# Order of the first strip's projections in a fused window-attention and depthwise-convolution kernel

## The chip, the cores and the metric

The kernel runs on one core of a Trainium2 chip. The metric is device time in microseconds (us): the median of a few executions of the same program. Engines are named TensorE (PE in the profile, its weight loads PEld), VectorE (DVE), ScalarE (ACT), GpSimd (POOL) and SyncE (SP), which here only issues transfers.

## The reference

The input x has 16 images of 56 x 56 tokens with 384 channels, in float32. Two layers follow each other, each with a residual.

```python
# layer 0: shifted-window attention on a group norm of x (32 groups)
qkv = roll(gn(x)) @ w_qkv.T                    # 12 heads of 32 channels, windows of 7 x 7 tokens
score = q @ k.T / sqrt(32) + rel_pos + masks
out = softmax(score) @ v
x = x + roll_back(out @ w_out.T + b_out)
# layer 1: depthwise 3 x 3 convolution with binarised weights on a group norm
x = x + depthwise(gn(x), sign(clip(w)))
```

The mean and variance of a group run over the whole image, so the attention of an image starts only when all of it has been read.

## The kernel before, in words

**Tiling.** An image is cut into 8 strips of 7 rows (`NS`); a strip `s` holds 8 windows, or 392 tokens (`ST`), and the whole run has 128 strips. A strip is worked on in two units of four windows each (`UPS`, `UW`); `u` counts units over the run. Channels lie on partitions in three blocks of 128 (`NC`), so the projections of a strip are six blocks of queries and keys and three of values, each block three products of 128 x 128 by 128 x 392 that add up in one bank of PSUM. Of each such float32 product the profile shows two records.

**Functions of one strip.**
- `normalize(s)` (ScalarE, L463) writes the normalised strip into `xn`, of which there is one buffer. It has to wait until the projections of the strip before have read it.
- `query_key(s, m)` (TensorE, L474) makes one block of queries or keys in a bank `pq`; ScalarE copies it to `qk` (L481).
- `value(s, m)` (TensorE, L487) makes a block of values in a bank `pv`; ScalarE copies it to `vt` (L494).
- `turn(s, m)` (VectorE, L498) transposes that block in squares of 32 x 32 from `vt` to `vq`.
- `by_key(s, part)` (SP, L510) carries `vq` to the tile `v`, in which keys lie on partitions. It issues eight transfers for each of its two parts, sixteen for a strip; each reads what all three turns of the strip wrote.

**Functions of one unit.**
- `scores(u)` (TensorE, L529) writes queries times keys into the score banks, of which there is one set.
- `softmax(u)` (VectorE, L546) adds the bias to them and writes `e`; the bias tile was made before, by `add_bias` (VectorE, L230), out of `rel` and `mask`, which POOL loads (L210, L213, L218).
- `exponential(u)` (ScalarE, L564) takes the exponential of `e`.
- `add_up(u)` (TensorE, L599) sums it over the keys, `invert(u)` (ScalarE and VectorE, L637 to L640) makes the reciprocal.
- `attend(u)` (TensorE, L619) multiplies `e` with `v` into two banks `po`, 96 small products; ScalarE copies them (L629) and `divide(u)` (VectorE, L647) scales them.
- `project(s, m)` (TensorE, L658, every second unit) makes the output projection, to which VectorE adds x (L666).

**What sets the order.** The whole program is under `tc.manual_schedule()`: each engine does its instructions in the order in which the Python code emits them, and waits at each one for the data and buffers it needs. `all_units` is the written-out order. It first emits the first strip by hand, and then runs a loop over units. In the loop `heavy(u)` gives six slots of projection work for the next strip: values and their turns in the first unit of a strip, with `by_key` near its end, and the rest of queries and keys in the second. The scores and the softmax of the next unit are emitted between the slots, and the unit's own sums and `attend` after slot 0:

```python
for m in range(NC):
    if half == 0 and more:
        todo[m].append((value, (s + 1, m)))
        todo[m + 1].append((turn, (s + 1, m)))
        todo[NC + m].append((query_key, (s + 1, m)))
```

Light work (the convolution of the image before, loads of the next image) is put into the slots by due times that `plan` hands out with `at(when, f, ...)`. `fetch_halves` (POOL, L421) loads strips of the next image into `xl`, and `turn_halves` (VectorE, L438) takes them up; the first 24 of these loads are issued in unit 0. In the queues of POOL and SP they and `by_key` stand where the code emits them, too.

Ahead of `all_units` the program reads the first image, loads weights and bias, gathers the statistics (through DRAM, SP L287 and L289) and normalises strip 0. `all_units` stands twice in the program; the second call, with `fast` false, lies under a condition on the numbers' range.

Of the kernel before, what the change touches and what calls it, by code (L numbers as in the profile page):

```python
# [34 lines left out]
def kernel(  # L35
# [17 lines left out]
    NC = C // P  # L53
# [39 lines left out]
    def bank(name):  # L93
        return ps.tile([P, 512], F32, tag="mm", name=name)
# [365 lines left out]
    def normalize(s):  # L460
        coef = coefs[0, s // NS]
        for c in range(NC):
            nc.scalar.activation(  # L463
                xn[:, c, :, :T],
                xs[s][:, c, :].rearrange("p (w t) -> p w t", t=T),
                AF.Identity,
                bias=coef[:, c, 1:2],
                scale=coef[:, c, 0:1],
            )

    def query_key(s, m):
        pq = bank(f"pq_{s}_{m}")
        for c in range(NC):
            nc.tensor.matmul(  # L474
                pq[:, :ST].rearrange("p (w t) -> p w t", t=T),
                wq_t[:, c, m * P : (m + 1) * P],
                xn[:, c, :, :T],
                start=(c == 0),
                stop=(c == NC - 1),
            )  # L480
        nc.scalar.copy(qk[:, m, :ST], pq[:, :ST])  # L481

    def value(s, m):

        pv = bank(f"pv_{s}_{m}")
        for c in range(NC):
            nc.tensor.matmul(  # L487
                pv[:, :ST].rearrange("p (w t) -> p w t", t=T),
                wq_t[:, c, 2 * C + m * P : 2 * C + (m + 1) * P],
                xn[:, c, :, :T],  # L490
                start=(c == 0),
                stop=(c == NC - 1),
            )
        nc.scalar.copy(vt[:, m, :, :T], pv[:, :ST].rearrange("p (w t) -> p w t", t=T))  # L494

    def turn(s, m):

        nc.vector.transpose(  # L498
            vq[:, :, :, m].rearrange("p h n d -> p n h d"),
            vt[:, m].rearrange("p (n w) (j b) -> p n (w j) b", w=2, b=D),  # L500
        )

    def by_key(s, part):

        if part == 0:
            vs[s] = vpool.tile([P, NW // 2, C], F32, tag="v", name=f"v_{s}")
        v = vs[s]
        for half in range(2 * part, 2 * part + 2):
            for i in range(HPC):
                nc.sync.dma_start(  # L510
                    v[half * D : (half + 1) * D].rearrange("k n (m c) -> k (n m) c", m=NC)[:, :, i * D : (i + 1) * D],
                    vq[i * D : (i + 1) * D, half].rearrange("k n m d -> k (n m) d"),
                )

    def scores(u, fast):


        s, n = divmod(u, UPS)
        pp = score_banks
        rows = T if fast else HT  # L520
        for j in range(NC):
            for r in range(2):
                for k in range(2 * HPC):
                    i, w = k % HPC, (k + k // HPC) % 2
                    part = slice(i * D, (i + 1) * D)
                    q0 = (n * UW + 2 * r + w) * T
                    row, col = (w, r) if fast else (r, w)
                    k0 = (2 * j + col) * T
                    nc.tensor.matmul(  # L529
                        pp[row * HT : row * HT + rows, i, k0 : k0 + T],  # L530
                        qk[part, NC * fast + j, q0 : q0 + rows],
                        qk[part, NC * (not fast) + j, q0 : q0 + T],
                        start=True,
                        stop=True,
                    )
        raw[u] = pp

    def softmax(u, fast):

        s = u // UPS  # L540
        pp = raw[u]
        e = es.rearrange("k (i j) w q -> k i (j w) q", i=HPC)[:, :, :, :T]
        if fast:
            flat = es.rearrange("k h w q -> k (h w q)")[:, : NH * 2 * T]
            e = flat.rearrange("k (i n q) -> k i n q", i=HPC, q=T)
        nc.vector.scalar_tensor_tensor(  # L546
            e,
            pp[:, :, : NC * 2 * T].rearrange("q i (n k) -> q i n k", k=T),
            QSCALE,
            bias[:, int(s % NS == NS - 1)].rearrange("q (i j) w k -> q i (j w) k", i=HPC),  # L550
            ALU.mult,
            ALU.add,
        )
        if fast:
            return
        e = es.rearrange("q h w k -> q (h w) k")[:, :, :T]
        top = small.tile([P, 2 * NH], F32, tag="top", name=f"top_{u}")
        nc.vector.tensor_reduce(top, e, AX.X, ALU.max)
        nc.vector.tensor_tensor(e, e, top.unsqueeze(2).to_broadcast([P, 2 * NH, T]), ALU.subtract)

    def exponential(u, fast):
        if fast:
            flat = es.rearrange("k h w q -> k (h w q)")[:, : NH * 2 * T]
            nc.scalar.activation(flat, flat, AF.Exp, accum_out=reach[:, 0, u : u + 1])  # L564
            return
        e = es.rearrange("q h w k -> q (h w) k")[:, :, :T]
        nc.scalar.activation(e, e, AF.Exp)
        total = small.tile([P, 2 * NH], F32, tag="total", name=f"total_{u}")
        nc.vector.tensor_reduce(total, e, AX.X, ALU.add)
        inv = small.tile([P, 2 * NH], F32, tag="inv", name=f"inv_{u}")  # L570
        nc.vector.reciprocal(inv, total)
        nc.vector.tensor_tensor(e, e, inv.unsqueeze(2).to_broadcast([P, 2 * NH, T]), ALU.mult)
# [366 lines left out]
    def heavy(u):  # L939

        s, half = divmod(u, UPS)
        todo = [[] for _ in range(2 * NC)]
        more = s + 1 < B * NS
# [5 lines that stand above are left out]
            if half and more:  # L949
                todo[m].append((query_key, (s + 1, NC + m)))  # L950
            if half:
                todo[NC + m].append((project, (s, m)))
        if more and not half:
            for part in range(2):
                todo[NC + 2 * part].append((by_key, (s + 1, part)))
        if half and s + 2 < B * NS:
            todo[NC + 1].append((normalize, (s + 2,)))
        return todo
# [5 lines left out]
    def plan(last_queue):  # L964
        for b in range(1, B):
            plan_load(b)
            plan_conv(b - 1, NU * b, 2.6 if b < B - 1 else 1.95, 3, 0.4, nc.gpsimd)
        at(B * NU - 6, fetch_late)
        for t in range(9):
            at(B * NU - 5 + 0.3 * t, diagonal, t)  # L970
        plan_last(B - 1, B * NU)

    def all_units(fast):
        for m in range(2 * NC):
            query_key(0, m)
        scores(0, fast)
        softmax(0, fast)
        for m in range(NC):
            value(0, m)
        normalize(1)  # L980
        exponential(0, fast)
        for m in range(NC):
            turn(0, m)
        for part in range(2):
            by_key(0, part)
        plan(nc.sync)
        for u in range(B * NU):
            todo = heavy(u)
            light = [(w, f, a) for w, f, a in sorted(side.pop(u, []), key=lambda i: i[0])]
            more = u + 1 < B * NU  # L990

            then = NC if u % UPS else NC - 1
            for i in range(len(todo)):
                run(todo[i])
                if i == 0:
                    if fast:
                        add_up(u)
                    else:
                        for j in range(NC):
                            transpose(u, j)  # L1000
                    if fast:
                        invert(u)
                    attend(u, fast)
                    if fast:
                        divide(u)
                if i == then and more:
                    scores(u + 1, fast)
                    softmax(u + 1, fast)
                if i == then + 1 and more:
                    exponential(u + 1, fast)  # L1010
                while light and light[0][0] - u <= (i + 1) / len(todo):
                    _, g, a = light.pop(0)
                    g(*a)
            for _, g, a in light:
                g(*a)
        for _, g, a in sorted((i for u in side for i in side[u]), key=lambda i: i[0]):
            g(*a)
        side.clear()
# [110 lines left out]
```

## Time and profile before

| what | value |
| --- | --- |
| time, median of 3 runs | 4079.17 us (4078.88 to 4080.06) |
| the profiled execution's own time | 4081.16 us |
| span of its trace | 4079.4 us |
| instructions | 144987 |
| TensorE busy | 3981.1 us |
| VectorE busy | 3495.8 us |
| ScalarE busy | 2231.7 us |
| GpSimd busy | 1870.2 us |
| mean granted TensorE clock | 0.991 |
| moved by DMA | 438.93 MB, 108 GB/s on average |

The span starts with the first recorded instruction of the program and ends with the last; the profiled execution's own time holds what lies around it as well. Times in the timeline and in the chain of waits count from the start of the span. A line of the timeline gives start, duration, engine, line, operation, the tiles it writes and reads, the number of records that are merged into it, and, in brackets, the idle time of the engine ahead of it with what ended it. In a table of slices each engine's busy time stands with its number of instructions, and after the five engines come the granted TensorE clock (1.00 is full speed), the mean busy share of the 16 DMA engines, and GB/s. The name of a releaser is inferred from semaphores, and can be that of another transfer which used the same semaphore.

### The profile page before, as it was taken

To read this page: it belongs to the slowest core of one execution; us is meant where nothing else is said; L and a number is where in the kernel's file an instruction comes from. 1 tells how busy PE (TensorE), PEld (TensorE's weight loads), DVE (VectorE), ACT (ScalarE), POOL (GpSimd) and SP (SyncE) were. 2 spreads that over 40 slices of the span, in tenths; PEclk is the share of its full clock that TensorE was granted. 3 is DMA by queue.
4 is the path that set the end of the run, shared out by engine and by line. 5 is a ranking of instruction groups with operands and counts; after the bars stand their busy time and mean duration, and the time that the engine had idled before them with its cause. 6 is when DMAs were issued, how large, how long until landed. Compare 5 with 4: busy or idle time off the path is not lost.

```text
span 4079.4 us, 144987 instructions
## 1 busy us (share of the span) xinstructions
PE 3981.1 (98%) x63161; PEld 2447.1 (60%) x63161; DVE 3495.8 (86%) x3712; ACT 2231.7 (55%) x4654; POOL 1870.2 (46%) x3165
## 2 busy tenths in 40 slices
PE   5999999999999999999999999999999999999997
PEld 3666666656656666566666666666566566666656
DVE  4555989889898998989889898998989889898897
ACT  2555646555565655656555565655656556565552
POOL 5444535545453554545445452554545455452100
PEclk8999999999999999999999999999999999999998
DMA  4434556655665665556665665655556565664544
GB/s 95 78 62 90 112 102 127 107 109 107 114 114 111 117 111 108 111 99 128 108 116 104 113 117 105 117 117 101 115 101 123 105 124 104 108 123 79 108 102 110
DMA packets 1523990, 438.93 MB, mean 108 GB/s; under 512 B 1458970, under 2 KB 1473979, under 8 KB 1523346
## 3 DMA queue, kind: packets, MB, share of 16 engines
q1 hardware_dynamic: 1432680, 267.66, 38.9%
q0 software_dynamic: 87648, 159.12, 16.4%
q8 instruction: 500, 8.19, 0.9%
q10 hardware_dynamic: 3018, 2.78, 0.3%
q14 instruction: 144, 1.18, 0.1%
HBM read 169.63 MB, written 158.46 MB: 80 GB/s over the span
## 4 chain that ended last, share of the span: by engine, by line
PE 46%; issue 16%; POOL 12%; DVE 12%; DMA 7%; SPq 4%; ACT 2%; DVEq 0%; ACTq 0%; POOLq 0%
PE pq L474 19%; PE pv L487 10%; PE py L658 8%; POOL xl L421 8%; DVE o L786 5%; PE score_banks L529 3%; PE po L619 3%; SPq L510 3%; DMA xl<-in_x_dram 2%; PE score_banks L599 2%; DMA mvd<-mv 2%; DVE e L546 1%; POOL dev L270 1%; DMA gt<-mvd 1%; DVE xt L438 1%
## 5 line engine op out<-in xcount | busy, mean ns | idle before, releaser
L474 PE MATMUL pq<-xn,wq_t 128*128 128x392 f32 x4608 | 1586.7, 497 | 0.1
L421 POOL DMA_DIRECT2D xl<-in_x_dram x1980 | 1329.3, 722 | 153.8 <-DVE xt L438 94.2
L786 DVE SCALAR_TENSOR_TENSOR o<-hp,dw_t,o 128x1568 f32<-128x1568 f32 x752 | 1378.4, 1833 | 5.7 <-DVE o L786 0.5
L474 PEld LDWEIGHTS pq<-xn,wq_t 128*128 128x128 f32 x4608 | 846.1, 188 | 596.1 <-issue 1.4
L487 PE MATMUL pv<-xn,wq_t 128*128 128x392 f32 x2304 | 815.9, 497 | 9.8 <-DVE y L666 8.6
L658 PE MATMUL py<-ot,wo_t 128*128 128x392 f32 x2304 | 818.2, 500 | 4.8 <-DVE ot L647 3.8
L481 ACT COPY qk<-pq 128x392 f32<-128x392 f32 x768 | 368.4, 482 | 609.6 <-PE pq L474 609.3
L678 POOL COPY y<-y 128x63 f32<-128x63 f32 x128 | 59.4, 464 | 1280.5 <-DVE y L666 1280.5
L487 PEld LDWEIGHTS pv<-xn,wq_t 128*128 128x128 f32 x2304 | 424.2, 189 | 309.9 <-DVE y L666 10.4
L658 PEld LDWEIGHTS py<-ot,wo_t 128*128 128x128 f32 x2304 | 425.8, 190 | 306.5 <-DVE ot L647 20.1
L564 ACT ACTIVATE e<-e 128x1176 f32<-128x1176 f32 x256 | 303.3, 1185 | 462.5 <-DVE e L546 461.4
L639 DVE SCALAR_TENSOR_TENSOR ln<-score_banks,inv 128x588 f32<-128x588 f32 x256 | 195.9, 765 | 349.2 <-ACT inv L638 349.2
L494 ACT COPY vt<-pv 128x392 f32<-128x392 f32 x384 | 188.8, 492 | 393.0 <-PE pv L487 392.1
L619 PEld LDWEIGHTS po<-e,v 49*32 49x32 f32 x24576 | 352.2, 105 | 60.4 <-issue 14.3
L619 PE MATMUL po<-e,v 49*32 49x49 f32 x24576 | 347.1, 212 | 13.4 <-DMA v<-vq 11.9
L546 DVE SCALAR_TENSOR_TENSOR e<-score_banks,bias 128x1176 f32<-128x1176 f32 x256 | 347.2, 1356 | 10.7 <-PE score_banks L529 10.7
L529 PEld LDWEIGHTS score_banks<-qk 32*49 32x49 f32 x24576 | 265.7, 118 | 145.4 <-issue 108.9
L450 ACT COPY x<-xt 128x196 f32<-128x196 f32 x720 | 225.5, 368 | 176.0 <-DVE xt L438 175.6
L529 PE MATMUL score_banks<-qk 32*49 32x49 f32 x24576 | 298.2, 218 | 2.6 <-DVE ln L639 2.2
L498 DVE STREAM_TRANSPOSE vq<-vt 128x512 f32<-128x512 f32 x384 | 265.6, 693 | 9.9 <-ACT vt L494 6.4
L463 ACT ACTIVATE xn<-x,coef 128x392 f32<-128x392 f32 x384 | 247.1, 711 | 13.3 <-DMA coef<-cod 13.3
L666 DVE TENSOR_TENSOR y<-py,x 128x392 f32<-128x392 f32 x384 | 213.3, 555 | 43.1 <-PE py L658 39.2
(174 smaller groups left out, 3279.3 us busy)
## 6 DMA issues: line engine op xcount, KB each, us to landing
v<-vq SPq DMA_DIRECT2D x2048, 48.0 KB
xb<-mid SPq DMA_DIRECT2D x90, 855.5 KB
out_dram<-o SPq DMA_DIRECT2D x736, 98.0 KB
mid<-y POOLq DMA_DIRECT2D x112, 619.5 KB
xl<-in_x_dram POOLq DMA_DIRECT2D x1260, 52.5 KB
mid<-y POOLq DMA_DIRECT2D x15, 354.0 KB
xl<-in_x_dram POOLq DMA_DIRECT2D x180, 28.0 KB
mid<-y POOLq DMA_DIRECT2D x15, 265.5 KB
```

Of the source, the lines that this page charges most:

```text
L421: nc.gpsimd.dma_start(xz[i * D + lo : i * D + hi, c, k : k + n, :], flat[token : token + n * (hi - lo)].rearrange("(k t) c -> t k c", k=n) ...
L463: nc.scalar.activation(xn[:, c, :, :T], xs[s][:, c, :].rearrange("p (w t) -> p w t", t=T), AF.Identity, bias=coef[:, c, 1:2], scale=coef[: ...
L474: nc.tensor.matmul(pq[:, :ST].rearrange("p (w t) -> p w t", t=T), wq_t[:, c, m * P : (m + 1) * P], xn[:, c, :, :T], start=(c == 0), stop=( ...
L481: nc.scalar.copy(qk[:, m, :ST], pq[:, :ST])
L487: nc.tensor.matmul(pv[:, :ST].rearrange("p (w t) -> p w t", t=T), wq_t[:, c, 2 * C + m * P : 2 * C + (m + 1) * P], xn[:, c, :, :T], start= ...
L498: nc.vector.transpose(vq[:, :, :, m].rearrange("p h n d -> p n h d"), vt[:, m].rearrange("p (n w) (j b) -> p n (w j) b", w=2, b=D),)
L529: nc.tensor.matmul(pp[row * HT : row * HT + rows, i, k0 : k0 + T], qk[part, NC * fast + j, q0 : q0 + rows], qk[part, NC * (not fast) + j, ...
L546: nc.vector.scalar_tensor_tensor(e, pp[:, :, : NC * 2 * T].rearrange("q i (n k) -> q i n k", k=T), QSCALE, bias[:, int(s % NS == NS - 1)]. ...
L564: nc.scalar.activation(flat, flat, AF.Exp, accum_out=reach[:, 0, u : u + 1])
L619: nc.tensor.matmul(po[w][i * D : (i + 1) * D, (2 * j + r) * T : (2 * j + r + 1) * T], vs[s][keys, n * 2 + r, h * D : (h + 1) * D], by_head ...
L658: nc.tensor.matmul(py[:, :ST], wo_t[:, c, m * P : (m + 1) * P], ots[s][:, c, :], start=(c == 0), stop=(c == NC - 1),)
L786: nc.vector.scalar_tensor_tensor(acc, by_half(hp[:, dy : dy + BR, dx : dx + W]), dw_t[:, c, t : t + 1], acc, ALU.mult, ALU.add)
```

## The change

The blocks with which `all_units` starts, for strip 0, are put in another order. Before, queries and keys came first, then the scores and softmax of unit 0, the values, `normalize(1)`, the exponential of unit 0, the turns, and `by_key`. After, each value block is emitted with its turn behind it, then come both parts of `by_key`, then queries and keys, scores, softmax, `normalize(1)` and the exponential. No call is added or removed, and the loop over units is as it was.

```diff
     def all_units(fast):
+        for m in range(NC):
+            value(0, m)
+            turn(0, m)
+        for part in range(2):
+            by_key(0, part)
         for m in range(2 * NC):
             query_key(0, m)
         scores(0, fast)
         softmax(0, fast)
-        for m in range(NC):
-            value(0, m)
         normalize(1)
         exponential(0, fast)
-        for m in range(NC):
-            turn(0, m)
-        for part in range(2):
-            by_key(0, part)
         plan(nc.sync)
```

## Prediction, made before the result was known

> **What bounds the kernel now.** I read the page first, then the list of TensorE's waits, then the timeline and the chain of waits around the strip that the change touches, then slices of 1 us there.
>
> The page's first part says which engine the whole run hangs on:
>
> ```profile
> PE 3981.1 (98%) x63161; PEld 2447.1 (60%) x63161; DVE 3495.8 (86%) x3712; ACT 2231.7 (55%) x4654; POOL 1870.2 (46%) x3165
> ```
>
> TensorE is idle for only 4079.4 - 3981.1 = 98 us. The waits of TensorE say where some of that lies; the second fence is the same view limited to 300 to 3800 us.
>
> ```profile
> PE po L619 <- DMA v<-vq: 11.9, 15, 5.4
> ...
> PE pv L487 <- ACT xn L463: 1.2, 1, 1.2
> ```
>
> ```profile
> PE pv L487 <- DVE y L666: 8.6, 13, 0.7
> PE po L619 <- DMA v<-vq: 4.0, 11, 0.6
> ```
>
> Of the 11.9 us that `attend` (po, L619) waits for the values' transfers, 4.0 lie in the long middle part; the rest (7.9) is the first unit. In 3500 us of middle TensorE waits under 14 us in all, so whatever TensorE gains at the start it keeps: nothing there has slack that could swallow it. The timeline of the start (start, duration, engine, line):
>
> ```profile
> 60.27 13.78 PE L474 MATMUL pq<-xn,wq_t 128*128 128x392 f32 x36
> ...
> 66.85 5.85 DVE L230 TENSOR_TENSOR bias<-rel,mask 128x147 f32<-128x147 f32 x16 [6.44 <-DMA xl<-in_x_dram]
> ...
> 75.05 6.19 PE L487 MATMUL pv<-xn,wq_t 128*128 128x392 f32 x18
> ...
> 84.81 0.73 PE L599 MATMUL score_banks<-e,ones 49*32 49x294 f32 x16
> ...
> 96.43 6.57 PE L487 MATMUL pv<-xn,wq_t 128*128 128x392 f32 x12
> ...
> 128.94 4.22 PE L487 MATMUL pv<-xn,wq_t 128*128 128x392 f32 x12
> ```
>
> The reader is to see three things. TensorE's sums (L599) are done at 85.54, and the next dense work starts after `attend` at 96.43. The same twelve records of `value` take 6.57 us after that hole and 4.22 us later: the clock had fallen. And VectorE adds the bias until 72.70. The chain of waits names what fills the hole:
>
> ```profile
> 81.81 0.72 DVE vq L498
> 82.55 0.76 SPq L510
> ...
> 93.07 2.11 DMA v<-vq
> 95.22 1.28 PE po L619 x76
> ```
>
> `turn` of the last block ends at 82.53; SP then issues the 16 transfers of `by_key` one by one, the last at 93.07, which lands 2.11 us later: 12.63 us from first issue to last landing. The slices tell the clock (7th number) and the DMA share (8th):
>
> ```profile
> 86.00:87.00 1.00, 0.00 (x0) 0.00 (x0) 0.00 (x0) 0.97 (x2) 0.00 (x0) 1.00 0.63 93
> 88.00:89.00 1.00, 0.00 (x0) 0.00 (x0) 0.79 (x2) 0.00 (x0) 0.00 (x0) 0.50 0.33 49
> ```
>
> **What the Trainium skill says.** "TensorE: Matmul & The Clock Gate", Part 1, has a clock at half after an idle window of about 3.4 us, back after a busy one, with windows that run free of the program. The trace agrees: half clock from about 87.5 to 101.2. It also shows that a window need not be quite idle: TensorE worked some 1.4 us between 84.1 and 87.5. "DMA: Bandwidth & Descriptors", Latency and other measured facts, gives a fixed cost of about 2 us a transfer; here 2.11 us. "Trainium Kernel Development and Optimization", Key Constraints, says that transfers issued from SP and POOL run on the same 16 DMA engines and interleave. That bears on the change, which moves `by_key` under POOL's fetch of x.
>
> **The change, part by part.** It removes and adds no instruction; three blocks of TensorE and what hangs on each change places.
>
> *TensorE's order.* Before: queries and keys 13.78, scores 1.07, values 6.14, ending at 81.24. After: values, queries and keys, scores. The same work at the same clocks must end at about 81.3 again. The first block pays for the cold clock and the arrival of xn: eighteen products took 13.78 where twice the nine of `value` would be 12.38, so 1.40 goes to whoever is first. Values then end at 60.27 + 6.19 + 1.40 = 67.86, queries and keys at 80.24, scores at 81.3. Cost nothing.
>
> *ScalarE's queue.* Three vt copies of 0.49 now stand before the six qk copies, each under products that take about 2 us per block. `normalize(1)` waits for the last reader of xn, now the last key block (80.24) instead of the last value block (81.24), so it comes 1.0 us earlier.
>
> *VectorE's queue.* The vt copies are done at about 68.4, but `turn` stands behind the sixteen additions of the bias in a queue that keeps its order. Those wait until 66.85 for rel and mask (the profile names POOL's later transfer, but L230 reads only these two) and run to 72.70. Three turns of 0.71 with their gaps: 72.70 + 2.2 = 74.9. That is the new start of `by_key`, 82.53 - 74.9 = 7.65 us earlier. Behind the turns on VectorE stands the softmax of unit 0; it is ready only when the scores end (81.3), so the turns cost it nothing while the bias is done by 79.
>
> *SP's queue.* All 16 issues of `by_key` move too. Ahead of them is only the coefficients' load (57.37), and nothing else is on SP until the next strip. Last issue 74.9 + 10.52 = 85.4, last landing 87.55, if the train keeps its pace.
>
> *The collision.* POOL issues 24 fetches of x from 64.94 to 81.67. Before, the train started after them; now 7 of its 12.6 us lie beside them. Alone the fetches hold the DMA engines at 0.39 (65 to 82 us), the train with its tail 0.45 (83 to 95). The sum, 0.84, is under one. A later strip shows both together: from 137 to 149 us, with 12 fetches, share 0.85, SP's 16 issues took 11.33 us where the uncontended ones run from 82.55 to 93.69, 11.14. Lower bound: nothing. Upper bound: SP's train at 1602 to 1617 us, beside stores, took 8 issues in 6.65 and 8 in 6.72 where 5.3 is normal, so +2 us here with slower landings. I take 0.5, since the last 4 us of the train have the DMA engines alone.
>
> *What is late next.* Without the values' wait TensorE would be ready for `attend` when? Softmax at 81.4 to 82.8, exponential at 82.85 (before 83.50), sums 1.31 later at 84.16, done at 84.9. The values land at 87.55 to 88, so they still end the wait; the rest of the hole is about 3 us instead of 10. `attend` ends 1.28 after the last landing: 88.85, before 96.50; gain 7.65, with the collision 7.15.
>
> *The clock.* The hole cost 6.57 - 4.22 = 2.35 us more in slow products. A hole of 3 us with some of `attend`'s products in it fits inside a window or is shared by two. Bounds: nothing saved (0) and all saved (2.35). I take 2.35: in any window at least a third would be busy, and the window before it is full. But the fall at 87.5 after a window about 40% busy shows that this is not certain.
>
> *Sum:* 7.65 - 0.5 + 2.35 = 9.5 us. The profiled execution took 4081.16 (span 4079.4 and 1.8 around it): 4071.7. The median of the timed runs is 2.0 under that, so 4079.17 - 9.5 = **4069.7 us**.
>
> **Rivals.** *A, smaller gain:* the collision costs its 2 us, the clock falls nonetheless, or both: gains of 5.6 to 8, 4071.2 to 4073.5; taken as 4072.5. For it: the share of 0.85, where any further load saturates; the fall after a 40% window. *B, given back:* the wait moves to something that doesn't come earlier with TensorE, as the fetched x for the next batch, which `turn_halves` takes at 116.91. Against it: those fetches are issued by 81.67, 27 us before even the earlier need. Gain 0: 4079.2. *C, slower:* `by_key`'s train and POOL's fetches choke each other, because every issue of SP from the ninth on waits for an older transfer to land. It decides when the train takes over 95.2 - 74.9 = 20.3 us instead of 12.6. At double the pace, 16 x 1.31 + 2.1 = 23.1, it lands at 98.0: +2.8, 4082.0; to lose 0.2% it would have to take 28.5. For it: single issues of 1.4 to 2 us on SP; against it the 11.33 of a train under the same fetches.
>
> **How the numbers follow.** Forecast 0.74, A 0.16, B 0.05, C 0.05. A measurement of this kernel can tell about 0.2%, 8.2 us, from no change: below 4071.0 is faster. The forecast's cases (8.2 to 11) are on that side, and a little of A: 0.75. Most of A, all of B and the nearer part of C are within 0.2%: 0.22. C's tail: 0.03. The low end takes the full gain with no collision, 10.0, and 1.5 for a shift of windows and of the small waits of the middle (0.7 at most each): 4067.7. The high end takes A whole: 4074.0.
>
> **What would show it.** First L510 at about 74.9, last near 85.5, sixteen of them in 11 to 12 us (right); `turn` directly behind the bias at 72.7; softmax of unit 0 at 81.4, as before the sums; TensorE's wait for v near 3 us; `value` after `attend` in 4.2 us, without half clock. It is wrong if v lands after 90, if the clock is half at 89 to 92, if the turns wait for something other than the bias, or if the shift at 130 us isn't found at 3900 us.

## The result and the profile after

The changed kernel takes 4071.55 us (median of 15 runs, 4068.01 to 4074.75), the kernel before 4079.27 in the same measurement: 7.7 us less, ratio 0.998 with a 95% interval of 0.9972 to 0.9988. Two more measurements, each beside runs of the kernel before on the same chip, gave 0.9981 (0.9973 to 0.9989; 8.4 us) and 0.9977 (0.9967 to 0.9986; 9.4 us). The same kernel differs by about 4 us from one chip to another, so medians are compared within one measurement, on one chip. The profiled execution took 4072.83 us, with a span of 4071.0.

The page's first part: TensorE's busy time hardly changed (3981.1 before), the span did.

```profile
PE 3978.3 (98%) x63161; PEld 2445.6 (60%) x63161; DVE 3495.6 (86%) x3712; ACT 2236.0 (55%) x4654; POOL 1876.6 (46%) x3165
```

TensorE's waits over the whole run, and then in 300 to 3800 us:

```profile
PE po L619 <- DMA v<-vq: 7.3, 16, 2.4
```

```profile
PE pv L487 <- DVE y L666: 8.4, 13, 0.9
PE po L619 <- DMA v<-vq: 5.0, 15, 0.9
```

The wait for v was 11.9 us in all; outside the middle it fell from 7.9 to 7.3 - 5.0 = 2.3, and the longest single wait from 5.4 to 2.4. The middle waits nearly as before: all of TensorE's listed waits there add up to 15.4 us, against 13.8. The timeline of the start:

```profile
59.11 7.71 PE L487 MATMUL pv<-xn,wq_t 128*128 128x392 f32 x18
...
65.73 5.86 DVE L230 TENSOR_TENSOR bias<-rel,mask 128x147 f32<-128x147 f32 x16 [6.47 <-DMA mask<-in_wmask_dram]
...
66.66 12.01 PE L474 MATMUL pq<-xn,wq_t 128*128 128x392 f32 x36
...
71.50 1.89 DVE L498 STREAM_TRANSPOSE vq<-vt 128x512 f32<-128x512 f32 x3
...
82.57 0.73 PE L599 MATMUL score_banks<-e,ones 49*32 49x294 f32 x16 [0.46 <-ACT e L564]
...
85.68 2.10 PE L619 MATMUL po<-e,v 49*32 49x49 f32 x94 [2.35 <-DMA v<-vq]
...
87.71 5.09 PE L487 MATMUL pv<-xn,wq_t 128*128 128x392 f32 x12
```

Three turns run in one piece directly behind the bias. The hole between the sums and `attend` is 2.35 us. But `value` behind it still takes 5.09 us, not 4.22: the clock fell again. The chain of waits and the slices (clock in the 7th column of numbers):

```profile
71.59 1.81 DVE vq L498 x3
73.42 0.76 SPq L510
...
82.37 3.18 DMA v<-vq
85.68 2.10 PE po L619 x90
```

```profile
86.00:87.00 1.00, 1.00 (x51) 0.97 (x52) 0.58 (x1) 0.00 (x0) 0.00 (x0) 0.55 0.03 4
88.00:89.00 1.00, 1.00 (x2) 0.55 (x2) 0.45 (x1) 0.52 (x2) 0.00 (x0) 0.50 0.00 0
90.00:91.00 1.00, 1.00 (x5) 0.56 (x4) 0.00 (x0) 0.14 (x1) 0.00 (x0) 1.00 0.00 0
```

Before, the half clock lasted from 87.5 to 101.2; now from about 86.1 to 89.5. In the second and third trace of the changed kernel it lasted from 88.4 to 91.8 and from 87.7 to 91.1.

The first projection starts at a slightly different place in each trace (58 to 61 us), through loads that the change doesn't touch. So the start is compared by counting from that first record of L474 or L487. All numbers below are us, each from one profiled execution; "train" is the first by_key of strip 0, from its first issue to its last landing by the trace's semaphores, and the last column is the time from the end of `attend` of unit 0 to the sums of unit 1, which holds a fixed piece of TensorE work. The other rows are the experiments of the next section.

| kernel | train starts | train takes | attend 0 ends | sums 1 start | attend 0 to sums 1 |
| --- | --- | --- | --- | --- | --- |
| before | 22.28 | 12.63 | 36.23 | 51.83 | 15.60 |
| before, second trace | 23.18 | 12.64 | 37.14 | 51.50 | 14.36 |
| after | 14.31 | 13.04 | 28.67 | 42.79 | 14.12 |
| after, second trace | 14.68 | 13.24 | 29.14 | 44.08 | 14.94 |
| after, third trace | 14.60 | 13.38 | 29.10 | 44.04 | 14.94 |
| values first, carry late | 24.37 | 12.59 | 38.28 | 53.16 | 14.88 |
| turns ahead of the bias | 9.06 | 15.58 | 25.69 | 38.93 | 13.24 |
| the same, second trace | 9.52 | 15.73 | 26.28 | 39.52 | 13.24 |
| fetches after the train | 14.64 | 12.75 | 28.51 | 43.22 | 14.71 |
| before, kept busy | 22.29 | 12.54 | 35.86 | 49.10 | 13.24 |
| values after three key blocks | 15.37 | 13.32 | 30.01 | 45.60 | 15.59 |
| the same, second trace | 16.39 | 13.53 | 31.24 | 45.54 | 14.30 |
| train twice | 14.79 | 23.85 | 39.96 | 54.91 | 14.95 |

### The profile page after: what moved, and what is told of

Its sections match the earlier page's. It is cut to its first block, busy times and chain, and to the rows that moved or that the text cites. A ratio compares the mean times of both kernels' runs of the same rounds, so it can differ in the third digit from the quotient of the medians.

```text
span 4071.0 us, 144984 instructions
## 1 busy us (share of the span) xinstructions
PE 3978.3 (98%) x63161; PEld 2445.6 (60%) x63161; DVE 3495.6 (86%) x3712; ACT 2236.0 (55%) x4654; POOL 1876.6 (46%) x3165
## 4 chain that ended last, share of the span: by engine, by line
PE 33%; issue 22%; POOL 18%; DVE 12%; DMA 9%; SPq 3%; ACT 2%; DVEq 0%; ACTq 0%; POOLq 0%
PE pq L474 14%; POOL xl L421 12%; PE pv L487 7%; PE py L658 6%; DVE o L786 6%; SPq L510 3%; PE score_banks L529 2%; PE po L619 2%; DMA mvd<-mv 2%; DMA xl<-in_x_dram 2%; PE score_banks L599 1%; POOL dev L270 1%; DMA mid<-y 1%; DVE e L546 1%; DMA gt<-mvd 1%
## 5 line engine op out<-in xcount | busy, mean ns | idle before, releaser
L474 PE MATMUL pq<-xn,wq_t 128*128 128x392 f32 x4608 | 1584.9, 496 | 0.4 <-issue 0.4
L474 PEld LDWEIGHTS pq<-xn,wq_t 128*128 128x128 f32 x4608 | 845.5, 188 | 595.9 <-issue 0.8
L487 PE MATMUL pv<-xn,wq_t 128*128 128x392 f32 x2304 | 817.4, 498 | 8.5 <-DVE y L666 8.4
L487 PEld LDWEIGHTS pv<-xn,wq_t 128*128 128x128 f32 x2304 | 425.2, 189 | 308.8 <-DVE y L666 10.1
L546 DVE SCALAR_TENSOR_TENSOR e<-score_banks,bias 128x1176 f32<-128x1176 f32 x256 | 347.4, 1357 | 14.6 <-PE score_banks L529 14.6
```

The costliest lines, as they stand in the source:

```text
L474: nc.tensor.matmul(pq[:, :ST].rearrange("p (w t) -> p w t", t=T), wq_t[:, c, m * P : (m + 1) * P], xn[:, c, :, :T], start=(c == 0), stop=( ...
L487: nc.tensor.matmul(pv[:, :ST].rearrange("p (w t) -> p w t", t=T), wq_t[:, c, 2 * C + m * P : 2 * C + (m + 1) * P], xn[:, c, :, :T], start= ...
L546: nc.vector.scalar_tensor_tensor(e, pp[:, :, : NC * 2 * T].rearrange("q i (n k) -> q i n k", k=T), QSCALE, bias[:, int(s % NS == NS - 1)]. ...
```

## The experiments

The theory under test is that of the prediction: the gain is the earlier landing of v, which the start of the train decides, and that in turn the bias on VectorE; TensorE's order by itself gives nothing. Rivals are that the order does it (with `normalize(1)` 1 us earlier), that POOL's fetches hold the train, and that the clock has a large share. The cuts of code show each edit against the changed kernel, only those of "Before, kept busy" against the kernel before; `...` stands for lines left out.

**Values first, carry late.** One part of the change alone: the value products move, their turns and `by_key` don't.

```diff
         for m in range(NC):
             value(0, m)
-            turn(0, m)
-        for part in range(2):
-            by_key(0, part)
...
         exponential(0, fast)
+        for m in range(NC):
+            turn(0, m)
+        for part in range(2):
+            by_key(0, part)
```

> Only the three value products stand first; the turns and by_key stay at their old place behind the softmax of unit 0. Carry theory (the gain comes from by_key starting earlier): softmax then runs at 81.4 to 82.8 and the three turns behind it, so by_key starts near 85.0, 2.4 us later than before, and the kernel is 2.4 us slower than before (about 4081.7 against 4079.3), with the clock lost as before. Order theory (the gain comes from TensorE's order and from normalize(1) coming 1 us earlier): about 1 to 8 us faster than before.

Measured: 4082.46 against 4080.18 us, ratio 1.0005 (0.9997 to 1.0013). No gain; a loss of the expected size, though the interval takes in none. The train starts at 24.37, later than in both traces of before, because the turns now stand behind the softmax:

```profile
79.64 1.38 DVE L546 SCALAR_TENSOR_TENSOR e<-score_banks,bias 128x1176 f32<-128x1176 f32 x1 [8.52 <-PE score_banks L529]
80.94 1.89 DVE L498 STREAM_TRANSPOSE vq<-vt 128x512 f32<-128x512 f32 x3
```

TensorE's waits at 60 to 100 us:

```profile
PE po L619 <- DMA v<-vq: 10.6, 4, 5.4
```

The wait for v is longer than the 7.9 of before, although TensorE had made the values about 13 us earlier. The order theory falls.

**Turns ahead of the bias.** The bound that the prediction named for the new start is taken away: the value block is emitted before the bias additions.

```diff
         load_depthwise()
-        add_bias(True)
         normalize(0)
+        first_values()          # values, turns and by_key of strip 0
+        add_bias(True)
         all_units(True)
```

> As the changed kernel, but values, turns and by_key are emitted ahead of the bias additions. Carry theory: the last turn follows the last vt copy (66.9 in the changed kernel's trace, 7.75 after the first value product) and ends 0.8 later; by_key starts some 5.7 us earlier than in the changed kernel, its last landing (15.7 us behind the bound of 86.5 now) comes at about 80 to 81.5, before the sums are done, and the hole ahead of attend goes: 2.4 us of wait and 0.9 us of half clock, so 3 to 3.5 us faster than the changed kernel, some 11 to 12.5 faster than before. The bias additions end some 2 us later, at 73 to 74, still ahead of the scores at 79.7. Collision theory (POOL's fetches hold the train): by_key now lies wholly beside the fetches and stretches beyond 15 us, v lands no earlier than 83 and the gain over the changed kernel is under 2 us.

Measured: 4068.36 against 4080.18 us, ratio 0.9971 (0.9961 to 0.9982). Its timeline:

```profile
67.28 0.71 DVE L498 STREAM_TRANSPOSE vq<-vt 128x512 f32<-128x512 f32 x1 [1.26 <-ACT vt L494]
67.92 5.82 DVE L230 TENSOR_TENSOR bias<-rel,mask 128x147 f32<-128x147 f32 x16
...
82.54 0.73 PE L599 MATMUL score_banks<-e,ones 49*32 49x294 f32 x16 [0.53 <-ACT e L564]
...
83.06 1.58 PE L619 MATMUL po<-e,v 49*32 49x49 f32 x96
...
84.57 4.22 PE L487 MATMUL pv<-xn,wq_t 128*128 128x392 f32 x12
```

`attend` follows the sums in one piece of 96, and `value` runs at full clock: the hole is gone. The train starts 5.3 us earlier than in the changed kernel and, with all its issues beside POOL's fetches, takes 15.6 us instead of 13.0. So v lands at 24.64, only 2.7 us earlier, later than expected; that is still in time, since the last products of `attend` need the last transfers. The collision is real, and it is hidden here.

**Fetches after the train.** The suspected contention is taken away by making POOL read a word of each quarter of v before its 24 fetches.

```diff
         exponential(0, fast)
+        held = small.tile([P, 1], F32, tag="held", name="held", bufs=1)
+        for half in range(4):
+            part = slice(half * D, (half + 1) * D)
+            nc.gpsimd.tensor_copy(held[part], vs[0][part, 0, C - 1 : C])
         plan(nc.sync)
```

> As the changed kernel, but POOL first reads a word of each quarter of v and only then issues its 24 fetches, so that the train of by_key has the DMA engines alone. Carry theory with a small collision: the train takes 12.6 us from first issue to last landing in place of 13.0, v lands 0.4 us earlier, and the time is within 0.5 us of the changed kernel, if the later fetches still land before turn_halves takes them at 106.7. Collision theory: 2 us or more faster than the changed kernel. If the fetches now come too late, TensorE shows a wait at its first projections of units 1 or 2 and the kernel is slower by that.

Measured: 4069.8 against 4080.18 us, ratio 0.9975 (0.9965 to 0.9986), not to be told from the changed kernel's 0.9977 to 0.9981, which was not measured beside it. The intervals are some us wide, so the times alone can't decide between a small collision and one of 2 us; the trace does. In it the train takes 12.75 us instead of 13.04 to 13.38. The collision of the change costs 0.3 to 0.6 us; the prediction had 0.5. No wait for the later fetches appears: `attend` 0 to the sums of unit 1 is 14.71.

**Before, kept busy.** The clock's share alone: twelve products that nobody reads fill the hole of the kernel before.

```diff
                     if fast:
                         invert(u)
+                    if u == 0:
+                        warm = bank("warm")
+                        for n in range(12):
+                            nc.tensor.matmul(warm[:, :ST]..., wq_t[:, n % NC, :P], xn[:, n % NC, :, :T],
+                                             start=(n == 0), stop=(n == 11))
                     attend(u, fast)
```

> The kernel before, with twelve products of 128x128 by 128x392 that nobody reads put between the sums and attend of unit 0 (7.9 us of work in a hole of 9.7). Clock theory: TensorE stays at full clock, value after attend takes 4.2 instead of 6.57 us, and the kernel is 2 to 2.4 us faster than before though it does more work. If the half clock costs nothing: same as before. If the extra products end after v has landed (93.4 against 95.2 expected): slower by the difference.

Measured: 4077.91 against 4080.18 us, ratio 0.9996 (0.9988 to 1.0005): 2.3 us by the medians, not clear of no change. The trace is plain:

```profile
83.90 8.17 PE L1006 MATMUL warm<-xn,wq_t 128*128 128x392 f32 x24
92.00 0.70 PE L619 MATMUL po<-e,v 49*32 49x49 f32 x10
...
94.48 4.22 PE L487 MATMUL pv<-xn,wq_t 128*128 128x392 f32 x12
```

With TensorE kept busy the clock stays, and the last column of the table is 13.24, the same as where the hole is gone. So 13.24 is that stretch at full clock, and what a trace has above it is the price of the half clock: 2.36 and 1.12 in the two traces of before, 0.88, 1.70 and 1.70 in the three of after.

**Train twice.** The suspected cost is doubled: all sixteen transfers are issued a second time with the same data.

```diff
-        for part in range(2):
+        for part in (0, 1, 0, 1):
             by_key(0, part)
```

(`by_key` keeps the tile of the first pass.)

> As the changed kernel, but all sixteen transfers of the first by_key are issued twice (same data, so the output is the same). Carry theory: sixteen more issues of 0.66 us put the last landing 10.5 us later, 3 us later than in the kernel before; the hole ahead of attend is longer than before and the clock falls in it, so the kernel is 2 to 4 us slower than before and 10 to 12 slower than the changed kernel. If the gain does not hang on when v lands: as the changed kernel.

Measured: 4087.59 against 4083.57 us, ratio 1.0009 (1.0002 to 1.0015), and 12.4 us slower than the changed kernel in the same measurement. The train takes 23.85 us, 10.6 more, and the wait for v at 60 to 100 us is longer than in any other trace:

```profile
PE po L619 <- DMA v<-vq: 11.3, 4, 5.8
```

In this and the other experiments the time follows the landing of v to within about 2 us, on both sides of the kernel before; the one exception is the first measurement of the three key blocks, below.

**The changed kernel and the turns ahead of the bias once more**, beside each other on one chip.

> The changed kernel once more, beside the kernels of this call: about 4071.5, as measured. The sum at the start of the trace (9.0 us by unit 1, counted from the first projection) says 8 to 9 us under the kernel before; if the middle of the run gives some of it back on average, 7 or less.

> The turns ahead of the bias once more, beside the changed kernel on the same chip. From its trace: 3.85 us ahead of the changed kernel at the sums of unit 1, counted from the first projection (2.98 of wait, 0.87 of half clock). Carry theory: 3 to 4 us faster than the changed kernel. If such a lead is lost in the rest of the run: no difference between the two.

Measured: 4075.21 and 4071.23 us against 4083.57: ratios 0.9981 and 0.9971 (0.996 to 0.9981). The lead of 4.0 us is the 3 to 4 that was expected.

**Values after three key blocks.** One size of the order: how late may the values stand on TensorE?

```diff
+        for m in range(NC):
+            query_key(0, m)
         for m in range(NC):
             value(0, m)
             turn(0, m)
         for part in range(2):
             by_key(0, part)
-        for m in range(2 * NC):
+        for m in range(NC, 2 * NC):
             query_key(0, m)
```

> As the changed kernel, but three of the six blocks of queries and keys stand ahead of the values (values end 6 us later on TensorE, at about 14.0 after the first product). Bias theory (the turns wait for the bias additions, not for TensorE): the bias still ends at 12.5 after the first product, the last turn waits only for the last vt copy, by_key starts 0.5 to 1 us later than in the changed kernel, and the time is within 1 us of it. Order theory (values must be first on TensorE): 4 to 6 us slower than the changed kernel.

Measured: 4079.31 us, ratio 0.9993 (0.9984 to 1.0001), 4.1 slower than the changed kernel, a miss. The trace has the train only 0.7 us later than the changed kernel measured beside it (15.37 against 14.68) and the sums of unit 1 1.5 later. So it was run again, with the changed kernel and the kernel before for a trace of its own:

> Three key blocks ahead of the values, once more: the first measurement had it 4.1 us slower than the changed kernel, where its trace accounts for 1.5 (0.7 later start of by_key, 0.2 elsewhere, 0.65 more half clock). If the trace is right, it comes out 1 to 2 us slower than the changed kernel; if there is something the trace didn't show, again 4.

> The changed kernel a third time, beside the next two. Ratio to before 0.998 as in the two measurements so far (0.9980 and 0.9981).

> The kernel before as a kernel of its own, for a trace from the same chip: ratio 1.000, the hole ahead of attend again about 9.7 us and the value pair behind it 5.8 to 6.6 us. Counted from the first projection, the changed kernel of this call should lead it by about 9 us at the sums of unit 1 and, if the rest of the run gives nothing back, by 7 to 11 at the last unit.

Measured: 4073.13, 4071.13 and 4079.43 us against 4080.49: ratios 0.998 (0.9972 to 0.9988), 0.9977 (0.9967 to 0.9986) and 0.9998 (0.9989 to 1.0007). Now it is 2.0 us slower than the changed kernel. Its timeline there:

```profile
72.38 0.71 DVE L498 STREAM_TRANSPOSE vq<-vt 128x512 f32<-128x512 f32 x1 [0.78 <-ACT vt L494]
...
74.36 0.71 DVE L498 STREAM_TRANSPOSE vq<-vt 128x512 f32<-128x512 f32 x1 [1.26 <-ACT vt L494]
75.10 12.04 SPq L510 DMA_DIRECT2D v<-vq  x16
```

The last two turns now wait for the copies of their values, not for the bias, so the train starts 1.8 us later than in the changed kernel beside it (0.7 in the first measurement, where only the last turn waited so). Three key blocks are just past the slack; TensorE's order matters only from there. What made the first measurement 2.6 us worse than its trace stays open; its runs were spread from 4072.75 to 4087.35.

Does the rest of the run give the gain back? In the two traces of this measurement, counted from the first projection, the changed kernel leads the kernel before by 7.5 us at the sums of unit 1 (44.04 against 51.50), by 7.0 at unit 128 (1976.9 and 1983.9) and by 6.2 at the last unit (3906.8 and 3913.0). Expected were about 9 and, at the last unit, 7 to 11: both came out lower. From the sums of unit 1 to those of the last unit the three traces of the changed kernel take 3862.8, 3864.4 and 3866.8 us, with TensorE idle for 26.8 to 28.8 us, and the two of before 3861.5 and 3861.9, with 24.5 and 24.8. So each of these traces of the changed kernel loses about 1 to 5 us of its lead on the way. The medians do not show such a loss: they differ by 7.7 to 9.4 us, and the start of the traces gives 8.0. Five single executions can't settle this, and whether a small part of the gain is given back stays open.

## Why the prediction was right, and where its sum was off

The predicted 4069.7 us stands against 4071.55, the gain of 9.5 against 7.7, 8.4 and 9.4 in three measurements. The first of them lies just under the 8.2 us that the prediction named as its bound for a difference, and inside the range of its rival A; the other two lie among the cases of its forecast. The stated range holds both, so that the number fell into it does not tell them apart. The terms do.

*TensorE's order costs nothing: right.* The scores end 1.14 after 78.60, 20.6 after the first projection; before it was 21.0 for the same three blocks (22.0 and 22.1 in the later traces, against 21.9). Moving the products alone gained nothing.

*The train starts behind the bias, 14.6 after the first projection (74.9): right.* Measured 14.31 to 14.68. That the bias is the bound, and not TensorE, is shown by both experiments at its sides: ahead of the bias the train starts at 9.06, and with three key blocks first it starts a little later, held by the copies.

*The train's pace: right.* 12.6 us plus 0.5 for the collision; 13.04 to 13.38, and 12.75 without the fetches. In the same trace the busy share of the DMA engines was 0.71 over 73 to 86 us.

```profile
73.00:86.00 13.00, 10.07 (x144) 5.70 (x142) 2.74 (x4) 6.76 (x13) 7.76 (x12) 1.00 0.71 116
```

*v still ends the wait, with 3 us of hole left, and `attend` ends 7.15 us earlier: right.* The hole is 2.35, and 1.8 in the two later traces. `attend` ends at 28.67 to 29.14 against 36.23 and 37.14, a lead of 7.7 between the means of the traces.

*The clock gives back 2.35: wrong in size.* This is the term that was mis-sized. The prediction took the clock as kept because a hole of 3 us holds some products and fits into a window. It fell in all three traces of the changed kernel, and `value` took 5.09 and twice 5.91 us instead of 4.22. In the second and third trace the clock was half at 89 to 91, which the prediction had named as a sign that it is wrong. In the first it fell at about 86.1, after a window of 3.4 us in which TensorE worked about 1.1 (82.68 to 83.34 and 85.68 to 86.09). That is 0.3 of the window, about the third that the prediction counted on. In the other two TensorE was busy for 2.28 and 2.16 of the 3.4 us before the fall, about two thirds, and the clock fell all the same. The slices of the second trace:

```profile
85.01:88.42 3.41, 2.28 (x96) 2.10 (x97) 1.54 (x2) 1.47 (x5) 0.00 (x0) 1.00 0.23 36
88.42:91.84 3.42, 3.42 (x6) 1.69 (x5) 1.39 (x2) 0.49 (x2) 0.00 (x0) 0.50 0.00 0
```

So the step that failed is the inference from some work in a window to a clock that stays. In one of three traces the fall costs 0.88, in two 1.70, against 2.36 and 1.12 in the two of before. So the clock's share is 1.74 - 1.43 = 0.3 between the means, and at best 1.5. The 2.35 was one trace's penalty; the other trace of before, with the same hole, has 1.2 less. "TensorE: Matmul & The Clock Gate", Part 1, says that the windows run free of the program. The traces agree: counted from the first projection, the fall came at 27.3 and 29.1 before, and at 27.0, 29.5 and 29.7 after. So a stall's clock cost should be read from several traces or as a range.

*Sum of what was measured:* 7.7 for the landing and 0.3 for the clock, 8.0 us, inside the 7.7 to 9.4 that the three measurements gave. That the third of them, 9.4, meets the predicted 9.5 is chance: in the two traces of that measurement the half clock cost not less after the change but more (1.70 against 1.12).

*Rivals.* A was half right: the collision cost no 2 us, but the clock fell nonetheless. That is the reason for which A expected a smaller gain. B, all of it given back, did not come; a small part is open, as said above. C, a train of 20.3 us or more, did not come: 13.0 to 13.4. The doubled train shows that its mechanism is sound: at 23.85 us v lands at 38.64, 3.7 later than in the first trace of before, and the kernel is 4.0 us slower.

The best version of the study puts the turns ahead of the bias: 0.9971 in both measurements, some 12 us under the kernel before.

## What to carry to other kernels

When a step is moved earlier, ask what stands ahead of it on each engine it passes: here the products could move by 13 us, but the transposes behind them were bound by an unrelated queue on VectorE, and two statements in another order there were worth 4 us more. Most of what a shorter stall gains early in this TensorE-bound run was still there at the end, so it pays to follow the chain from the stall to the first issue of a transfer, not only to its landing. A stall that is shortened but not removed can still cost the clock, even when TensorE works through most of the window around it.

## What the runs showed of the hardware

- The clock fell after windows that were far from idle: TensorE was busy for 1.3 of 3.4 us in the kernel before, for 1.1, 2.28 and 2.16 in the traces of the changed kernel. Kept busy through the hole, it did not lose the clock. Yet the busy time by the profile doesn't decide alone: after a window with 2.05 us (2532.4 to 2535.8 in the second trace of the changed kernel) and after one with 2.22 (79.2 to 82.6 in "Before, kept busy") the clock stayed. What decides stays open.
- Such a fall also happened once in the middle of the changed kernel's first trace, behind short waits for v (0.36, 0.49 and 0.16 us) and after 3.4 us in which TensorE was busy for 2.41. The slice shows the half clock, and the value pair there took 5.71 us instead of 4.22:

```profile
2192.00:2195.50 3.50, 3.50 (x52) 2.11 (x42) 3.10 (x4) 2.42 (x3) 0.76 (x2) 0.52 0.69 206
```

- SP issued a transfer of 48 KB every 0.66 us as a rule, whether or not POOL's fetches ran. A train alone took 12.5 to 12.8 us, one about half beside the fetches 13.0 to 13.4, one with all its issues beside them 15.6 and 15.7. In the changed kernel the time went into a single issue of the sixteen, which took 1.15, 1.34 and 1.43 us in its three traces; the last landing came 2.1 to 2.2 us after the last issue, as without contention. In the turns ahead of the bias the issues kept their pace (10.5 and 10.7 us from the first to the last, 10.5 before), and the last landing came 5.1 and 5.0 us after the last issue. Why the one issue is held is not shown.
